# A transformer block on one core: the last two token tiles of the input products, with the other order of parts and one more tile transposed there

## The chip, the cores and the metric

The kernel runs on one core of a Trainium2 chip. The core has five engines with instruction streams of their own: TensorE (PE, matrix products and transposes), VectorE (DVE), ScalarE (ACT), GpSimd (POOL) and SyncE (SP, which issues DMAs here). [...] The metric is the time of one execution on the device in microseconds, and the median over runs is what counts.

## The reference

The computation is one block of a diffusion transformer, in float32, for 2 batches of 2048 tokens with 576 features: 16 heads of 36 dimensions and a hidden layer of 2304.

```python
mod = silu(c) @ w_ada + b_ada                    # six rows of 576 per batch
xn = ln(x) * (1 + sc_msa) + sh_msa
q, k, v = split(xn @ w_qkv + b_qkv)              # 576 -> 3 * 576
q, k = ln(q), ln(k)                              # over the 36 dimensions of each head
o = softmax(q @ k.T / sqrt(36)) @ v              # per head
x = x + g_msa * (o @ w_proj + b_proj)
h = gelu((ln(x) * (1 + sc_mlp) + sh_mlp) @ w1 + b1)
x = x + g_mlp * (h @ w2 + b2)
```

## The kernel before

**Stages.** For each batch the input products (`inputs`), the attention (`attend`) and the output product (`outputs`) follow one another; the hidden layer comes for both batches at the end. The change lies where the input products end and the attention opens, so it acts twice.

**Input products.** The 2048 tokens are 16 tiles of 128 (NT = 16, numbered 0 to 15). For each tile there are three products, q, k and v (w = 0, 1, 2), of 128 tokens by 576 features each, in two halves of 288 columns. The 576 input features are four chunks of 128 and one of 64. So a product has a part of 128 rows (`whole`, L376: eight matmuls) and a part of 64 rows (`halved`, L387: two matmuls, on the two halves of the array's rows). For tiles 0 to 13 a loop (L972) puts the 64-row parts of q, k and v together. The last two tiles have a loop of their own (L1005), in which `two_products` (L394) takes the two parts in an order by its argument `turn`: 128 rows first where it is even, 64 rows first where it is odd. Below, product number n = 3t + w: products 42, 43, 44 belong to tile 14, and 45, 46, 47 to tile 15.

**What follows a product.** `biased` (L957) takes it out of PSUM on VectorE. When q and k of a tile are there, `centred` (L879) subtracts each head's mean on VectorE and squares on ScalarE. Later `head_scale` (L894) sums the squares (VectorE), takes the square root (ScalarE, L903), the reciprocal (VectorE) and multiplies (POOL, L907). Then the rows are normalised, and `by_feature` (L912) transposes the nine chunks of q and k on TensorE (L917) and takes them out of PSUM: chunks 4 to 8 on VectorE (L926), chunks 0 to 3 on ScalarE (L922). For tile 15 `centred` runs for q behind product 45 and for k behind product 46, and `head_scale` follows at once.

**Keys for the attention.** When a block of tiles has been transposed, `by_feature` also issues DMAs on SP (`take_k_block`, L806) that copy the first pair's keys to the layout of the attention. The split of the last four dimensions (`parted`, L787, on VectorE) is put on the list `taken`, and runs at the end of the next call of `by_feature`. Tiles 12 and 13 are one such block, tiles 14 and 15 the next.

**The last two tiles before the change.** In tile 14, behind k (product 43), come the five transposes of tile 15's normed input (`input_by_feature`, L853, with five activations on ScalarE, L365) and the nine of tile 12. In tile 15, behind q (product 45), come the nine of tile 13. Tiles 14 and 15 are transposed inside the attention: `last` (L937) makes a call of `by_feature` for some chunks only, in which VectorE takes out all of them.

**The attention.** It goes by steps (p, qb, g): pair of heads, block of 512 queries, group of keys. In each step TensorE makes 16 score banks in two sets of eight matmul pairs (L1049), ScalarE takes the exponentials (L1053), and TensorE multiplies the exponentials of the step before by v (L1062). `hooks` (L1247) maps a step to something that is called in it behind the values: (0, 0, 0) tile 14's chunks 4 to 8, (0, 0, 1) tile 15's, (0, 1, 0) tile 14's chunks 0 to 3, (0, 1, 1) tile 15's. Keys of tiles 12 to 15 are read from g = 2 on, and the last query block from qb = 3.

**PSUM.** The eight banks are four tiles of two banks (`s_tile`) in the input products and eight single banks (`bank`) in the attention. An allocation waits until the last reader of what lay there has finished.

**Order.** TensorE runs in the order of the program text throughout. VectorE does so in `inputs` and `attend`, POOL in `attend`. The order on ScalarE is made by the framework's planner, which runs the program in its own reckoning of time and gives a free engine the earliest instruction of the text that is ready.

Of the kernel before, what the change touches and what calls it, by code (L numbers as in the profile page):

```python
# [23 lines left out]
NKC = FULL + 1  # L24
# [7 lines left out]
def dit_block(  # L32
# [30 lines left out]
    NT = N // P  # L63
# [7 lines left out]
    NQK = 2 * C // P  # L71
# [14 lines left out]
    def s_tile():  # L86
        return psum["s"].tile([P, 2, 512], F32, tag="s", name="s")
# [273 lines left out]
    def modulated(dst, src, which, b, apart=False):  # L361

        t4, t1 = transposed(*src, apart)
        for k in range(NKC):
            nc.scalar.activation(  # L365
                dst[:, k, :],
                t4[:, k * P : (k + 1) * P] if k < FULL else t1[:, :P],
                AF.Identity,
                bias=mod[:, which, k, b : b + 1],
                scale=mod[:, which + 1, k, b : b + 1],  # L370
            )
# [22 lines left out]
    def two_products(outs, stationary, moving, turn):  # L394


        parts = (whole, halved) if turn % 2 == 0 else (halved, whole)
        for part in parts:
            part(outs, stationary, moving, part is parts[0])
# [325 lines left out]
    def block_of_small():  # L725
# [34 lines left out]
        parts = ident.rearrange("p (r a b) -> p r a b", a=2, b=2)  # L760
# [8 lines left out]
        def chunk(c, cols):  # L769
            return qo[:, c, cols] if c < NKC else kr[:, c - NKC, cols]  # L770
# [42 lines left out]
        def take_q(p, qb):  # L813
            i = qb % 2
            src = lambda c: slice(qb * BLK, (qb + 1) * BLK)
            rows_taken(nc.sync, qm[i], qe[i], range(2), p * 2 * HD, src, slice(0, BLK))
            return lambda: parted(qe[i], slice(0, P), low_q, sign_q)
# [32 lines left out]
        def input_rows(b, t, queue):  # L850
            return tile_normed(tile_loaded(x[b, t * P : (t + 1) * P, :], queue))

        def input_by_feature(b, rows, apart=False):  # L853
            xnt = xs["pool"].tile([P, NKC, P], F32, name="xnt", bufs=2)
            modulated(xnt, rows, 0, b, apart)
            return xnt
# [13 lines left out]
        def inputs(b, weights, work, xnt, loaded):  # L870
# [5 lines left out]
            def banks_of_two():  # L876
                return [bank for ps in (s_tile(), s_tile()) for bank in (ps[:, 0], ps[:, 1])]
# [34 lines left out]
            def by_feature(t, banks, chunks=range(NQK), all_on_vector=False):  # L912
                both, begun = normed[t], [*taken]
                taken.clear()
                parts = [(c, banks[i // 4][:, i % 4 * P : i % 4 * P + P]) for i, c in enumerate(chunks)]
                for c, ps in parts:
                    nc.tensor.transpose(ps, both[:, c * P : (c + 1) * P], ident)  # L917

                for c, ps in parts[::-1]:
                    dst = chunk(c, slice(t * P, (t + 1) * P))  # L920
                    if c < 4 and not all_on_vector:
                        nc.scalar.activation(  # L922
                            dst, ps, AF.Identity, bias=bias_qk[:, c : c + 1], scale=gain_qk[:, c : c + 1]
                        )
                    else:
                        nc.vector.tensor_scalar(  # L926
                            dst, ps, gain_qk[:, c : c + 1], bias_qk[:, c : c + 1], ALU.mult, ALU.add
                        )
                for do in begun:
                    do()  # L930
                if t == TPB - 1:
                    taken.append(take_q(0, 0))
                if t + 1 in key_tiles and NQK - 1 in chunks:
                    i = key_tiles.index(t + 1)
                    taken.append(take_k_block(*key_tiles[i - 1 : i + 1]))
# [7 lines left out]
            def next_rows(t):  # L943
                return tile_normed(loaded.pop(0)) if loaded else input_rows(b, t, nc.sync)
# [25 lines left out]
            rows = next_rows(1)  # L970
            before = None
            for t in range(NT - 2):  # L972
# [11 lines left out]
                ahead = input_by_feature(b, rows, t in ((0, 9), (0, 1))[b])  # L984
                rows = next_rows(t + 2)
# [19 lines left out]
            for t in range(NT - 2, NT):  # L1005
                both = work.tile([P, 2 * C], F32, name="both", bufs=3)
                for w in range(3):
                    ps, parts = product(w, xnt)
                    two_products(*parts, 3 * t + w)
                    biased(w, ps, t, both)  # L1010
                    if w == 0:
                        head_scale(t - 1, before)

                    if w == (1 if t % 2 == 0 else 0):
                        if t + 1 < NT:
                            ahead = input_by_feature(b, rows)
                        by_feature(t - 2, banks_of_two())

                    if t == NT - 1 and w < 2:
                        centred(both, w, w + 1)  # L1020
                    if t == NT - 1 and w == 1:
                        head_scale(t, both, ((0, 1), (1, 2)))
                if t + 1 < NT:
                    centred(both)
                before, xnt = both, ahead
# [185 lines left out]
        for b in range(B):  # L1211
            work, close_work = opened("work", side="right")
            with tc.manual_schedule(engines={mybir.EngineType.DVE}):
                last_inputs = inputs(b, weights, work, xnt, loaded)
            close_weights()
            att, close_att = opened("att")
            close_psum()
            close_psum = opened_psum(b=8)
            km[1] = att.tile([P, N // 2], F32, name="km1")
            qm[1] = att.tile([P, BLK], F32, name="qm1")  # L1220
            opening = {}

            def last_inputs_done():
                last_inputs(NT - 1, range(NKC - 1))
                close_work()

            def ada_opened():
                opening["ada"], opening["close"] = opened("ada_later", 2, side="right")
                opening["was"] = ada_weights(opening["ada"], GATES[0])
                opening["gates"] = gate_biases(opening["ada"], GATES[0], GATES[2])  # L1230

            def ada_gates():
                gates(opening["was"], opening["gates"], *GATES[:2])
                opening["was"] = ada_weights(opening["ada"], LATER[0])
                opening["biases"] = feature_biases(opening["ada"], LATER[0], nc.sync)

            def ada_feature_rows():
                opening["rows"] = feature_rows(opening["ada"], opening["was"], opening["biases"])

            def ada_features():  # L1240
                features(opening["rows"], LATER[1])
                opening["close"]()

            def output_opened():
                opening["wp"] = output_weights(b)

            hooks = {  # L1247
                (0, 0, 0): lambda: last_inputs(NT - 2, range(NKC - 1, NQK)),
                (0, 0, 1): lambda: last_inputs(NT - 1, range(NKC - 1, NQK)),
                (0, 1, 0): lambda: last_inputs(NT - 2, range(NKC - 1)),  # L1250
                (0, 1, 1): last_inputs_done,
                (4, 0, 1): output_opened,
            }
            hooks |= {
                (3 + t // NBLK, t % NBLK, 3): lambda t=t: residual_begun(b, t) for t in range(NT + 1)
            }
            if b == 0:
                hooks |= {
                    (0, 2, 1): ada_opened,
                    (1, 0, 2): ada_gates,  # L1260
                    (2, 0, 2): ada_feature_rows,
                    (2, 0, 3): ada_features,
                }
            with tc.manual_schedule(engines={mybir.EngineType.DVE, mybir.EngineType.Pool}):
                attend(b, att, hooks)
            close_att()
            close_psum()
            close_psum = opened_psum(s=4)
            wp, close_wp = opening["wp"]
            if b + 1 < B:  # L1270
                weights, close_weights = input_weights()
                between = {
                    9: [lambda: opening.update(rows=input_rows(b + 1, 0, nc.scalar))],
                    14: [lambda: opening.update(xnt=input_by_feature(b + 1, opening["rows"]))],
                }
                outputs(b, wp, between, spare)
                xnt = opening["xnt"]
                close_wp()
# [373 lines left out]
```

## Time and profile before

| | |
|---|---|
| median of 3 runs | 3221.94 us (3221.2 to 3221.95) |
| the profiled execution | 3220.86 us, of which 3219.0 us from first to last instruction |
| TensorE / VectorE / ScalarE / POOL busy | 99% / 45% / 46% / 11% |
| granted clock of TensorE | 1.00 |
| tile 14 begins, batch 0 / 1 | 229.22 / 1319.55 us |
| first scores, batch 0 / 1 | 259.21 / 1349.55 us |
| first values, batch 0 / 1 | 266.30 / 1356.63 us |

In the profile L12 is line 12 of the kernel. A line of a timeline has the start in us, the length in us, the engine, the line, the operation, output and input, their shapes, and how many such instructions were merged; brackets hold the idle time of the engine ahead of it and what ended it. A float32 matmul counts as two instructions of TensorE, and lengths overlap there, so differences of starts are read. Values of a step's start are the mark that is used for the attention's pace: two of them lie 5.98 us apart where nothing stands between.

### The profile page before, as it was taken

The numbers are of one execution on the slowest core, as the hardware profiler recorded it, in microseconds if no ns is written. First come the engines' busy times: TensorE is split into PE (matmuls) and PEld (weight loads), VectorE is DVE, ScalarE is ACT, GpSimd is POOL, SyncE is SP. The second block draws the span as 40 slices with busy tenths as digits, with TensorE's granted clock in tenths as the row PEclk, the third lists the DMA queues.
The fourth block names the chain that finished last, engine by engine and source line by source line (L and its number), as shares of the span: only waits on it lengthen the run. The fifth ranks groups of instructions, "written<-read, shape, count | busy, mean of one in ns | idle before, by whom it ended". The sixth has DMA issues, their size and how long they took to land.

```text
span 3219.0 us, 46999 instructions
## 1 busy us (share of the span) xinstructions
PE 3199.1 (99%) x18143; PEld 1883.2 (59%) x18143; DVE 1452.6 (45%) x2131; ACT 1495.2 (46%) x2952; POOL 355.2 (11%) x432
## 2 busy tenths in 40 slices
PE   8999999999999999999999999999999999999999
PEld 6774333333333777633333333368888888777777
DVE  4674333333333367633333333345555444455454
ACT  2335666676666033466666667633555552000000
POOL 1111000112110111200001111010000000111111
PEclk9999999999999999999999999999999999999999
DMA  4102212223221401111222222154322223333321
GB/s 131 30 26 68 74 33 69 63 72 87 69 82 33 145 23 31 30 54 43 48 48 68 63 71 72 44 176 158 119 87 91 91 80 119 145 132 111 118 103 38
DMA packets 129332, 253.16 MB, mean 79 GB/s; under 512 B 22979, under 2 KB 68492, under 8 KB 127052
## 3 DMA queue, kind: packets, MB, share of 16 engines
q1 hardware_dynamic: 105588, 182.07, 18.5%
q0 software_dynamic: 22640, 66.23, 7.4%
q8 instruction: 145, 2.38, 0.3%
q10 hardware_dynamic: 872, 1.77, 0.2%
q14 instruction: 87, 0.71, 0.1%
HBM read 135.40 MB, written 66.35 MB: 63 GB/s over the span
## 4 chain that ended last, share of the span: by engine, by line
PE 99%; DMA 1%; SPq 0%; DVE 0%; issue 0%; ACT 0%; DVEq 0%
PE b L1062 28%; PE b L1049 19%; PE s L379 16%; PE s L1564 15%; PE m L1405 12%; PE s L390 2%; PE m L1419 2%; PE one L1405 2%; PE s L917 1%; PE s L357 1%; PE t L1465 0%; DMA wq<-in_w_qkv_dram 0%; PE b L192 0%; PE b L917 0%; DMA km<-qo 0%; PE s L358 0%
## 5 line engine op out<-in xcount | busy, mean ns | idle before, releaser
L1053 ACT ACTIVATE pt<-b 128x512 f32<-128x512 f32 x2048 | 1057.7, 610 | 485.4 <-PE b L1062 272.0
L1062 PE MATMUL b<-pt,vt 128*64 128x512 f32 x4096 | 935.0, 598 | 0.0
L1062 PEld LDWEIGHTS b<-pt,vt 128*64 128x64 f32 x4096 | 271.8, 136 | 582.0 <-issue 438.2
L1049 PE MATMUL b<-qm,km 32*128 32x512 f32 x4096 | 566.7, 614 | 0.3 <-DMA km<-qo 0.3
L1110 DVE TENSOR_TENSOR ot<-b,ot 128x512 f32<-128x512 f32 x192 | 132.8, 692 | 653.1 <-PE b L1062 652.6
L1049 PE MATMUL b<-qe,ke 16*128 16x512 f32 x2048 | 423.0, 790 | 0.0
L379 PE MATMUL s<-wq,xnt 128*128 128x288 f32 x1536 | 391.4, 408 | 1.9 <-DMA wq<-in_w_qkv_dram 1.1
L1564 PE MATMUL s<-ws,as 128*128 128x288 f32 x1440 | 351.8, 406 | 0.0
L1049 PEld LDWEIGHTS b<-qm,km 32*128 32x128 f32 x4096 | 191.7, 184 | 269.3 <-ACT pt L1053 206.8
L379 PEld LDWEIGHTS s<-wq,xnt 128*128 128x128 f32 x1536 | 284.6, 190 | 86.5 <-issue 13.5
L1564 PEld LDWEIGHTS s<-ws,as 128*128 128x128 f32 x1440 | 273.6, 190 | 75.6
L1081 DVE RECIPROCAL den<-den 128x512 f32<-128x512 f32 x64 | 213.5, 3337 | 12.0 <-DMA den<-den_dram 12.0
L1405 PE MATMUL m<-xnt,wb 128*128 128x256 f32 x864 | 213.8, 383 | 0.0
L1405 PE MATMUL m<-s,wb 128*128 128x256 f32 x864 | 210.1, 379 | 0.2 <-DVE s L1375 0.2
L1108 DVE COPY ot<-b 128x512 f32<-128x512 f32 x64 | 44.3, 692 | 334.7 <-PE b L1062 334.7
L1405 PEld LDWEIGHTS m<-xnt,wb 128*128 128x128 f32 x864 | 159.1, 190 | 32.2 <-issue 11.9
L1405 PEld LDWEIGHTS m<-s,wb 128*128 128x128 f32 x864 | 164.1, 190 | 22.9 <-DVE s L1375 0.6
L1049 PEld LDWEIGHTS b<-qe,ke 16*128 16x128 f32 x2048 | 108.2, 184 | 114.3 <-issue 113.1
L1432 DVE TENSOR_TENSOR cs<-m,cs 128x512 f32<-128x512 f32 x72 | 49.7, 691 | 212.3 <-ACT cs L1431 150.9
L1564 PE MATMUL s<-ws,hidden 128*128 128x288 f32 x576 | 142.3, 406 | 0.0
L1542 DVE TENSOR_TENSOR as<-hidden 128x1152 f32<-128x1152 f32 x80 | 139.1, 1802 | 0.0
L1443 ACT ACTIVATE cs<-cs,b_sb 128x512 f32<-128x512 f32 x144 | 98.8, 719 | 68.2 <-DVE cs L1438 31.4
(174 smaller groups left out, 2521.0 us busy)
## 6 DMA issues: line engine op xcount, KB each, us to landing
gelu<-cs SPq DMA_DIRECT2D x144, 256.0 KB
hidden<-gelu SPq DMA_DIRECT2D x16, 2304.0 KB
den<-den_dram SPq DMA_DIRECT2D x128, 128.0 KB
x_dram<-kr POOLq DMA_DIRECT2D x48, 288.0 KB, 2.8
qm<-qo SPq DMA_DIRECT2D x192, 64.0 KB
kr<-in_x_dram POOLq DMA_DIRECT2D x32, 288.0 KB, 3.8
xr<-x_dram SPq DMA_DIRECT2D x32, 288.0 KB
out_dram<-y POOLq DMA_DIRECT2D x30, 288.0 KB, 3.9
```

Source lines behind the costliest of these rows:

```text
L379: nc.tensor.matmul(outs[a], stationary(k, a), moving(k, a), start=(first and k == 0), stop=(not first and k == FULL - 1),)
L390: nc.tensor.matmul(outs[a], stationary(FULL, a)[r], moving(FULL, a)[r], start=first, stop=not first)
L1049: nc.tensor.matmul(ps, k[r, keys], q[r, :], start=first, stop=not first)
L1053: nc.scalar.activation(pt[:, h, :], banks[2 * c + h], AF.Exp, scale=SCALE)
L1062: nc.tensor.matmul(acc[64 * h : 64 * h + 64, :], vt[:, v0 : v0 + 64], pt[:, h, :], start=pt is pts[0][0], stop=pt is pts[-1][0],)
L1081: nc.vector.reciprocal(den, den)
L1110: nc.vector.tensor_tensor(ot, acc, ot, ALU.add)
L1405: nc.tensor.matmul(out_m[m], wb[:, slot[m], k, f * P : (f + 1) * P], moving[m](k), start=k == 0 and (m == 1 or (first and m in (2, 5, 6))) ...
L1419: nc.tensor.matmul(out_m[m], w[r, f * P : (f + 1) * P], a[r, FULL, t * PAIR : (t + 1) * PAIR], start=first and m != 4, stop=not first and ...
L1443: nc.scalar.activation(part, part, AF.Gelu, bias=b1_sb[:, g : g + 1])
L1542: nc.vector.tensor_tensor(stationary[m], x_, y_, op)
L1564: nc.tensor.matmul(ms[m], stationary[m][:, f, :], ws[m][:, f, :], start=(f == 0), stop=(f == HF - 1))
```

## The change

In the last two tiles `turn` is one higher, so that products 42, 44 and 46 begin with the 64-row part and 43, 45 and 47 end with it. The transposes move: tile 15's input and tile 12's q and k stand behind product 42 in place of 43, tile 13's behind 44 in place of 45. Tile 14's nine transposes stand behind product 46, ahead of `centred` for tile 15's k; ScalarE takes out four of the nine and VectorE five. The two hooks that transposed tile 14 in the attention are gone; tile 15's stay.

```diff
@@ -1006,15 +1006,15 @@
                 for w in range(3):
                     ps, parts = product(w, xnt)
-                    two_products(*parts, 3 * t + w)
+                    two_products(*parts, 3 * t + w + 1)
                     biased(w, ps, t, both)
                     if w == 0:
                         head_scale(t - 1, before)
 
-                    if w == (1 if t % 2 == 0 else 0):
-                        if t + 1 < NT:
-                            ahead = input_by_feature(b, rows)
-                        by_feature(t - 2, banks_of_two())
+                    if t == NT - 2 and w == 0:
+                        ahead = input_by_feature(b, rows)
+                    if 3 * t + w in (3 * NT - 6, 3 * NT - 4, 3 * NT - 2):
+                        by_feature(t - 2 + (w > 0), banks_of_two())
 
                     if t == NT - 1 and w < 2:
                         centred(both, w, w + 1)
@@ -1245,9 +1245,7 @@
             hooks = {
-                (0, 0, 0): lambda: last_inputs(NT - 2, range(NKC - 1, NQK)),
                 (0, 0, 1): lambda: last_inputs(NT - 1, range(NKC - 1, NQK)),
-                (0, 1, 0): lambda: last_inputs(NT - 2, range(NKC - 1)),
                 (0, 1, 1): last_inputs_done,
                 (4, 0, 1): output_opened,
             }
```

## The prediction

> **What bounds the kernel now.** I read the page first.
>
> ```profile
> span 3219.0 us, 46999 instructions
> PE 3199.1 (99%) x18143; PEld 1883.2 (59%) x18143; DVE 1452.6 (45%) x2131; ACT 1495.2 (46%) x2952; POOL 355.2 (11%) x432
> PE 99%; DMA 1%; SPq 0%; DVE 0%; issue 0%; ACT 0%; DVEq 0%
> ```
>
> TensorE carries 99% of the chain that ended last. Time is won or lost only as TensorE time, and a microsecond lost in the middle stays lost. The change acts at two places per batch, the end of the input products and the opening of the attention, so I read TensorE's order of time there, for batch 1 (batch 0 looks alike).
>
> ```profile
> 1335.36 4.15 PE L379 MATMUL s<-wq,xnt 128*128 128x288 f32 x16
> 1339.34 1.15 PE L917 MATMUL s<-ident,both 128*128 128x128 f32 x9
> 1340.33 4.05 PE L379 MATMUL s<-wq,xnt 128*128 128x288 f32 x16
> 1344.30 1.24 PE L390 MATMUL s<-wq,xnt 64*128 64x288 f32 x8
> 1345.47 4.15 PE L379 MATMUL s<-wq,xnt 128*128 128x288 f32 x16
> 1349.55 1.14 PE L1049 MATMUL b<-qm,km 32*128 32x512 f32 x8
> ...
> 1352.28 0.77 PE L917 MATMUL b<-ident,both 128*128 128x128 f32 x5
> ...
> 1356.63 3.65 PE L1062 MATMUL b<-pt,vt 128*64 128x512 f32 x16
> ...
> 1377.38 3.65 PE L1062 MATMUL b<-pt,vt 128*64 128x512 f32 x16
> 1380.97 0.66 PE L917 MATMUL b<-ident,both 128*128 128x128 f32 x4
> ...
> 1384.40 3.65 PE L1062 MATMUL b<-pt,vt 128*64 128x512 f32 x16
> ```
>
> From start to start: a 128-row part of a product takes 3.98 us, a pair of 64-row parts 1.17, nine transposes 0.98. Input products run without a gap up to the first scores at 1349.55. From there to the first values it takes 7.08 us, though a set of scores costs 2.40 in the steady state (304.43 to 306.83) and two sets plus five transposes (0.70) would be 5.5. So the opening has slack. Who sets it shows on ScalarE and VectorE:
>
> ```profile
> 1349.53 0.32 ACT L903 ACTIVATE var<-var,eps 128x32 f32<-128x32 f32 x1 [0.82 <-DVE var L897]
> 1349.87 1.28 ACT L1053 ACT_TABLE_LOAD   x1
> 1351.16 4.03 ACT L1053 ACTIVATE pt<-b 128x512 f32<-128x512 f32 x8
> ```
>
> ```profile
> 1340.22 1.34 DVE L897 TENSOR_REDUCE var<-sq 128x32 f32<-128x1152 f32 x1
> 1342.02 0.35 DVE L905 RECIPROCAL inv<-var 128x32 f32<-128x32 f32 x1 [0.46 <-ACT var L903]
> ...
> 1347.91 1.58 DVE L897 TENSOR_REDUCE var<-sq 128x16 f32<-128x576 f32 x2
> ```
>
> The square root of tile 15 (L903) comes first, then the table load for Exp, then eight exponentials that free the eight PSUM banks one by one; the second set of scores can end only behind the last. The first values start 5.47 us after the first exponential in both batches (1351.16 to 1356.63; 260.83 to 266.30). The opening is thus set by that square root, not by TensorE.
>
> [...] Here three 64-row parts take 1.66 us and two 1.17: 0.49 each and about 0.19 for a run, a small cost.
>
> **The change, part by part** (batch 1, W a 128-row part, H a 64-row part, T transposes).
>
> *Parity.* Before: WH HW WH HW WH HW. After: HW WH HW WH HW WH. Two single H stand at the ends in place of one pair: the same matmuls, one run more, about +0.1 us (0 to 0.2, from 0.19). I count an H at 0.58, half the pair.
>
> *Tile 14's nine transposes among the products.* +0.98 in the products. On the other side, five leave the opening (0.70) and four leave a later step. That step takes 7.02 us against 5.98 for its free neighbour (1371.40 to 1377.38): 1.04 saved (batch 0: 1.05). The five in the opening save nothing, since they stand inside the slack that the exponentials set; if they weren't covered it would be 0.70.
>
> *Input transposes of tile 15 and tile 12's transposes one product sooner.* Same instructions. Five ScalarE activations (1.85 us) start about 4 us sooner; product 44 then waits for their PSUM tile, which they leave some 2 us ahead of it. Counted at nothing; 0.6 us if the planner puts them behind tile 13's square root.
>
> *T13 one product sooner.* Five SP DMAs for keys of tiles 12 and 13 (1343.58 to 1347.14 in issue) go about 5 us sooner. Nothing else of SP's stands between. Their split on VectorE (0.85 us, from 1354.80) now follows tile 14's evictions, 12 us after tile 13's; for tile 15's block the same data came within 6.7 us (1362.34 to 1369.05). No wait.
>
> *The wait that T14 brings.* It needs tile 14's normalised rows, whose chain begins behind T13's evictions on VectorE. From T13's start:
> - VectorE, ScalarE, POOL: 1.19 to the first eviction (1329.23 to 1330.42), 1.71 for five, 1.60 for mean (1335.69 to 1337.29), 1.45 to the square, 1.20 to the sum of squares (1324.40 to 1325.60), 1.80 to the reciprocal, 0.49 to POOL (1342.51), 2.12 for its multiplication: 11.56 us.
> - TensorE: T13 0.98, product 45 W 3.98, HH 1.17, 46 W 3.98: 10.11 us.
>
> T14 therefore waits 1.45 us (0.5 to 2.5: no T14 in this place is in the trace, and eight terms of about 0.1 doubt each add up). Behind it stand product 47 and the scores. T13 begins 15.22 us into the stage (0.58+3.98+0.55+0.98+3.98+1.17+3.98), at 1334.77, so T14 at 1346.33 and the scores at 1346.33+0.98+3.98+0.58 = 1351.87, 2.32 late.
>
> *What is behind T14 on VectorE.* Its five evictions stand ahead of tile 15's key half (L885 to L887) and of its sum of squares. From T14's start: 1.19, 1.71, 0.85 for the split, 1.00 for the mean (1346.24 to 1347.24), 0.67 to the sums of squares, 1.62 to the square root, 1.63 to the first exponential: 8.67 us, so 1355.00 against 1351.16. The exponentials are **3.84 us late**, and they set the first values. The scores' own 2.32 are inside this. The last matmuls behind the eighth exponential may be shorter, as the two banks of the five transposes no longer come last: I take −0.2 (0 to −0.45).
>
> *Sum.* 3.84 − 0.2 − 1.04 = 2.6 us a batch. In batch 0 tile 14 starts at 229.22 in place of 1319.55 and the same sums give 264.67 against 260.83, again 3.84. Two batches: **+5.2 us**. Against the profiled execution's 3220.86 (span 3219.0 and 1.86 around it) that is 3226.1; the median of the runs is 1.1 above that execution, so 3221.94 + 5.2 = **3227.1 us**, 0.16% up. About 0.2% (6.4 us) is what a measurement tells from no change, so this counts as the same.
>
> **The rivals.**
> 1. *Exponentials ahead of the square root: slower.* ScalarE's order is the planner's. By my times the first exponential has its scores at 1351.87+1.45 = 1353.32 (1.45 as from 1374.98 to 1376.43), and the square root its sums at 1353.37. If in the planner's reckoning one exponential comes first, ScalarE loads Exp at once after the last square (1352.55, exponentials from 1353.85), then the square root's table, then Exp again: 1.28+0.32+1.28 = 2.88 more among the eight. They end at 1360.76 in place of 1359.03, 1.73 later a batch; 5.2+3.5 = 8.7, **3230.6 us**. It decides as soon as one exponential stands ahead. For it: a margin of 0.05 us. Against: before, the root came first, by 1.5 us.
> 2. *The opening doesn't hang on the exponentials.* Then only the scores' 2.32 count, less 0.70 and 1.04: 0.6 a batch, **3223.1 us**. Against it: 5.47 twice alike. For it: the eight exponentials could be taken up by later slack.
> 3. *Another wait*, such as a PSUM tile held by late ScalarE evictions (0.6 us above, or more): about 1.5 a batch more, 3230.
>
> **How the numbers follow.** My forecast 0.5, rival 1 0.3, rival 2 0.1, rival 3 0.1. The forecast's own range is 3225.5 to 3229, from the wait's bounds and the 0.45. The range 3223.0 to 3231.5 takes in rivals 1 and 2. Slower by over 0.2%: all of rival 1, 0.12 of the forecast, most of rival 3, 0.5. Faster: only if neither wait appears and all transposes saved count, 0.02. Same: 0.48.
>
> **What would show it.** In the changed profile: TensorE idle of about 1.5 us ahead of the L917 group between the last two 128-row parts of the products, put down to POOL L907; scores some 2.3 us later; one table load in the opening, some 3.8 later, or three (rival 1); first values 5.3 to 5.5 after the first exponential; one step of 7.0 fewer. The forecast is wrong if T14 finds its rows ready and the square root isn't late, or if the exponentials are late and the values aren't.

## The result, and the profile after

The changed kernel takes **3227.39 us** (median of 17 runs, 3226.73 to 3229.3) against 3221.80 us for the kernel before, measured beside it (17 runs, 3220.1 to 3223.07): +5.6 us or 0.17% by the medians. The ratio of all the runs is 1.0019, with a 95% interval of 1.0012 to 1.0026. That is slower, and just inside the 0.2% that were counted as no change.

The profiled execution of the changed kernel took 3228.63 us, 1.2 above its median; that of before was 0.9 below its own. The two profiles therefore lie 7.8 us apart where the medians lie 5.6 apart. The 7.8 divide as follows, by the start of the first input product of each batch (18.79 and 1111.15 us before, 19.88 and 1116.14 after): 1.1 ahead of any product, where nothing was changed, 3.9 in batch 0 and 2.8 from batch 1 on. The page of the changed kernel, its first two lines and the chain that ended last:

```profile
span 3226.8 us, 47001 instructions
PE 3202.7 (99%) x18143; PEld 1885.6 (58%) x18143; DVE 1454.2 (45%) x2123; ACT 1497.7 (46%) x2960; POOL 354.5 (11%) x432
...
PE 97%; DVE 2%; ACT 0%; DMA 0%; SPq 0%; issue 0%; DVEq 0%; ACTq 0%
```

There are as many matmuls as before, but VectorE now has 2% of the chain, where it had 0%. (That is how long the chain runs through VectorE, not what was lost there.) TensorE's order of time in batch 1 shows where (start, duration, instruction; in brackets the idle time ahead of it and what ended it):

```profile
1339.96 1.15 PE L917 MATMUL s<-ident,both 128*128 128x128 f32 x9
1340.94 4.05 PE L379 MATMUL s<-wq,xnt 128*128 128x288 f32 x16
1344.92 1.24 PE L390 MATMUL s<-wq,xnt 64*128 64x288 f32 x8
1346.09 4.15 PE L379 MATMUL s<-wq,xnt 128*128 128x288 f32 x16
1351.47 1.20 PE L917 MATMUL s<-ident,both 128*128 128x128 f32 x9 [1.24 <-POOL both L907]
1352.51 4.05 PE L379 MATMUL s<-wq,xnt 128*128 128x288 f32 x16
1356.49 0.76 PE L390 MATMUL s<-wq,xnt 64*128 64x288 f32 x4
1357.17 1.14 PE L1049 MATMUL b<-qm,km 32*128 32x512 f32 x8
...
1365.73 3.65 PE L1062 MATMUL b<-pt,vt 128*64 128x512 f32 x16
```

T13 (1339.96), T14 (1351.47) with 1.24 us of idle time ahead of it, the scores, the first values. On VectorE, in the same stretch:

```profile
1349.07 0.69 DVE L885 TENSOR_REDUCE sums<-both 128x16 f32<-128x576 f32 x1
1349.79 1.65 DVE L886 TENSOR_SCALAR sums<-sums 128x16 f32<-128x16 f32 x1
1351.48 0.76 DVE L887 TENSOR_TENSOR both<-both,sums 128x576 f32<-128x576 f32 x1
1352.16 0.75 DVE L960 TENSOR_TENSOR both<-s,bq 128x576 f32<-128x576 f32 x1
1352.83 1.36 DVE L926 TENSOR_SCALAR kr<-s,gb_qk 128x128 f32<-128x128 f32 x4
1354.10 0.40 DVE L926 TENSOR_SCALAR qo<-s,gb_qk 128x128 f32<-128x128 f32 x1
```

The second line is the one that I had not looked for: a scaling of 16 numbers in each partition takes 1.65 us, where it takes 0.17 us elsewhere. What releases it stands in POOL's order of time, and what it leads to in ScalarE's:

```profile
1349.29 2.12 POOL L907 TENSOR_TENSOR both<-both,inv 128x1152 f32<-128x1152 f32 x1 [14.06 <-PE s L379]
```

```profile
1358.74 0.32 ACT L903 ACTIVATE var<-var,eps 128x32 f32<-128x32 f32 x1 [0.82 <-DVE var L897]
1359.08 1.28 ACT L1053 ACT_TABLE_LOAD   x1
1360.37 5.00 ACT L1053 ACTIVATE pt<-b 128x512 f32<-128x512 f32 x10
```

POOL multiplies tile 14's rows from 1349.29 to 1351.41, and L886 ends at 1351.44. There is one table load, behind the square root of tile 15, and ten exponentials follow it without a gap. Counted from the start of tile 14 (1319.55 before, 1324.63 after), the square root comes 29.98 us into the stage before and 34.11 after, the first exponential at 31.61 and 35.74: 4.13 us late.

### The profile page after: what moved, and what is told of

Its sections match the earlier page's. It is cut to its first block, busy times and chain, and to the rows that moved or that the text cites. A ratio compares the mean times of both kernels' runs of the same rounds, so it can differ in the third digit from the quotient of the medians.

```text
span 3226.8 us, 47001 instructions
## 1 busy us (share of the span) xinstructions
PE 3202.7 (99%) x18143; PEld 1885.6 (58%) x18143; DVE 1454.2 (45%) x2123; ACT 1497.7 (46%) x2960; POOL 354.5 (11%) x432
## 4 chain that ended last, share of the span: by engine, by line
PE 97%; DVE 2%; ACT 0%; DMA 0%; SPq 0%; issue 0%; DVEq 0%; ACTq 0%
PE b L1062 28%; PE b L1049 19%; PE s L1562 15%; PE s L379 14%; PE m L1403 12%; PE m L1417 2%; PE s L390 2%; PE one L1403 2%; PE s L917 1%; PE s L357 0%; PE t L1463 0%; DVE both L887 0%; DMA wa<-in_w_ada_dram 0%; DVE kr L926 0%; DVE sums L885 0%; PE b L192 0%
```

## The experiments

Two theories stood after the result. **W**: TensorE's wait ahead of T14 is what makes the opening late, as the prediction had it. **L**: VectorE is late by itself, since its own order of work has changed. Times "into the stage" are counted from the start of tile 14, as above, and come from the one profiled execution of each kernel. The experiments also ask which part of the change costs what. T12, T13 and so on are the transposes of those tiles; "the root" is the square root of tile 15.

**Is it the root that the opening hangs on?** In the kernel before, the two sums of squares of tile 15 are taken twice:

```
-                        head_scale(t, both, ((0, 1), (1, 2)))
+                        head_scale(t, both, ((0, 1), (1, 2), (0, 1), (1, 2)))
```

> The kernel before, with tile 15's two sums of squares taken twice on VectorE (1.58 us more ahead of its square root); TensorE's work is untouched. Theory A: first exponential and first values 1.6 us later in each batch, +3.2 us in all. Theory B: no change, 0 us.

Measured: 3223.81 us against 3221.18, ratio 1.0008 (1.0001 to 1.0015), +2.6. VectorE's order of time in this kernel:

```profile
1351.62 2.90 DVE L897 TENSOR_REDUCE var<-sq 128x16 f32<-128x576 f32 x4
```

It was 1.58 for two, so the two extra sums took 1.32 us and not the 1.58 that were expected. The root is 1.37 later in both batches (31.35 into the stage for 29.98), the first values are 1.37 later as well (38.45 for 37.08), and the time follows. The other side of the same claim is that five transposes in the opening cost nothing. They were left out of the kernel before, and the places that they would fill were zeroed:

```
-                (0, 0, 0): lambda: last_inputs(NT - 2, range(NKC - 1, NQK)),
+                (0, 0, 0): lambda: last_inputs(NT - 2, range(0)),
```

> The kernel before without tile 14's five transposes and evictions in the opening (its chunks 4 to 8 stay zero; the split of the keys of tiles 12 and 13 stays where it was). Theory A (the opening hangs on the exponentials behind tile 15's square root, so these five are hidden): 0 to -0.8 us against the kernel before, the latter if the last scores' tail is 0.4 us shorter a batch. Theory B (TensorE's own work sets the opening): -1.4 us.

Measured: 3221.39 against 3221.34, ratio 0.9999 (0.9991 to 1.0008), 0.0. That interval is some 5 us wide, so the time alone doesn't tell the two theories apart, and the trace shows that the run is no clean test. VectorE and ScalarE have in batch 1

```profile
1349.55 0.35 DVE L792 TENSOR_SCALAR high<-ke,part 64x256 fp32r<-64x256 f32 x1 [0.18 <-DMA ke<-kr]
```

```profile
1352.36 5.00 ACT L1055 ACTIVATE pt<-b 128x512 f32<-128x512 f32 x10
```

The split of the keys of tiles 12 and 13 (L792) did not stay where it was: it now runs between tile 15's two sums of squares, although it stands behind them in the program text, and puts the root off, by 0.44 us in batch 0 and 0.47 in batch 1. The first values come 0.33 and 0.36 us later than before, although TensorE has five transposes less to do. Behind the first exponential they come after 5.35 us in place of 5.47. So 0.12 of the 0.70 us show, and the rest lay inside the slack: the first values again follow the exponentials, and not TensorE's work.

**Wait or order?** In the changed kernel, T14 reads tile 13's rows, which have long been there, so TensorE need not wait:

```
-                both, begun = normed[t], [*taken]
+                both, begun = normed[t - 1 if t == NT - 2 else t], [*taken]
```

> The change, but tile 14's transposes read tile 13's rows, which are long ready (wrong values for tile 14): TensorE doesn't wait for POOL. Theory W (that wait is what makes everything behind it late): scores and square root about 1.4 us earlier a batch, -2.5 us against the change, so +3 us over the kernel before. Theory L (VectorE is held as long anyway, in the scaling of tile 15's sums, L886, which took 1.65 us in place of 0.17 and ended with POOL's multiplication of tile 14): scores 1.3 us earlier, square root and first exponential as late as in the change, time as the change, +5 to +5.6 us.

Measured: 3227.55 against 3221.34, ratio 1.0022 (1.0013 to 1.0031), +6.2: nothing is won. TensorE's, VectorE's and ScalarE's orders of time of this kernel:

```profile
1350.07 1.15 PE L917 MATMUL s<-ident,both 128*128 128x128 f32 x9
```

```profile
1349.80 1.66 DVE L886 TENSOR_SCALAR sums<-sums 128x16 f32<-128x16 f32 x1
```

```profile
1359.09 1.28 ACT L1053 ACT_TABLE_LOAD   x1
```

T14 starts 1.40 us sooner and the idle time ahead of it is gone, but L886 still takes 1.66 and the table load stands at 1359.09, where the change has it at 1359.08; in both batches the root is as far into the stage as in the change, within 0.02 us. W as it stands falls: the loss doesn't need TensorE's wait.

**Is it POOL's multiplication that holds VectorE?** In the changed kernel POOL multiplies the first half of tile 14 alone (the q half; k stays unscaled):

```
+                n = H if t == NT - 2 else 2 * H
-                    heads, heads, inv.unsqueeze(2).to_broadcast([P, 2 * H, HD]), ALU.mult
+                    heads[:, :n], heads[:, :n], inv[:, :n].unsqueeze(2).to_broadcast([P, n, HD]), ALU.mult
```

> The change, with POOL multiplying only the q half of tile 14 (its keys stay unscaled): 1.06 us less of POOL. Theories W and L both: transposes of tile 14, square root and first values 1.06 us earlier a batch, -2.1 us against the change. If something else holds VectorE and TensorE there (the PSUM tiles, the DMAs of the keys): 0.

Measured: 3225.54 against 3221.34, ratio 1.0013 (1.0006 to 1.0019), +4.2; 1.4 to 1.9 less than the change (by the differences, or by the medians themselves). POOL's and VectorE's orders of time here:

```profile
1345.27 1.15 POOL L908 TENSOR_TENSOR both<-both,inv 128x576 f32<-128x576 f32 x1 [14.06 <-PE s L379]
```

```profile
1345.77 0.68 DVE L886 TENSOR_SCALAR sums<-sums 128x16 f32<-128x16 f32 x1
```

POOL's operation ends at 1346.42, and L886 at 1346.45. Its length follows POOL's end. The interval overlaps that of the change, so the times alone don't prove the gain, but the traces have it: the root is 0.96 and 0.98 us earlier into the stage in batches 0 and 1 (34.09 and 33.13, for 35.05 and 34.11). Both theories had asked for that, as POOL releases T14 as well.

**What do tile 14's evictions cost?** In the changed kernel ScalarE takes all nine of them, so that none stands ahead of the root on VectorE:

```
-                    if c < 4 and not all_on_vector:
+                    if (c < 4 or t == NT - 2) and not all_on_vector:
```

> The change, with all nine chunks of tile 14 taken out of PSUM on ScalarE, so that only the split of the keys stands ahead of tile 15's keys on VectorE. If the evictions on VectorE are what puts the square root off (my step of 1.71 us): the square root waits for the last square on ScalarE behind nine evictions of 0.37 us in place of it, about 1 us earlier a batch, -2 us against the change. If they are not: 0 or slower than the change.

Measured: 3225.16 against 3221.34, ratio 1.0011 (1.0005 to 1.0018), +3.8, so 1.8 to 2.2 less than the change (again with overlapping intervals). TensorE's and ScalarE's orders of time:

```profile
1349.16 1.20 PE L917 MATMUL s<-ident,both 128*128 128x128 f32 x9 [1.24 <-POOL both L907]
```

```profile
1355.24 0.32 ACT L903 ACTIVATE var<-var,eps 128x32 f32<-128x32 f32 x1 [0.82 <-DVE var L897]
```

The wait ahead of T14 is still 1.24, but from T14 to the root it takes 6.08 us in place of 7.27, and the first values come 1.17 us sooner into the stage (39.93 for 41.10). Again the time follows the root and not TensorE's wait.

**Which part of the change makes VectorE meet POOL?** First the change without tile 14: the parity, and T12, T13 and the input transposes of tile 15 a product sooner.

```
-                    two_products(*parts, 3 * t + w)
+                    two_products(*parts, 3 * t + w + 1)
...
+                    if 3 * t + w in (3 * NT - 6, 3 * NT - 4):
+                        by_feature(t - 2 + (w > 0), banks_of_two())
```

> The other parity, and the transposes of tiles 12 and 13 and of tile 15's input one product sooner; tile 14 stays in the attention as before. Theory A (the loss comes from tile 14's transposes, through their wait and through tile 15's square root behind their evictions): a single run of 64-row parts more and a wait of product 43 for its PSUM tile in batch 0, 0.2 and 0.9 us, so 0.5 to 1.5 us over the kernel before, and one table load in the opening as late as before. Theory P (the single runs of 64-row parts cost most of it): 3 us or more over the kernel before.

Measured: 3229.25 against 3221.18, ratio 1.0026 (1.0016 to 1.0037), +8.1. Theory A had it too low. The number lies where theory P put it, 3 us or more, but theory P's reason still has to be tested. The orders of time of VectorE, POOL, ScalarE and TensorE:

```profile
1348.83 1.65 DVE L886 TENSOR_SCALAR sums<-sums 128x16 f32<-128x16 f32 x1
...
1355.96 0.69 DVE L963 TENSOR_TENSOR vt<-s,bq 128x576 f32<-128x576 f32 x1
```

```profile
1348.33 2.13 POOL L907 TENSOR_TENSOR both<-both,inv 128x1152 f32<-128x1152 f32 x1 [14.06 <-PE s L379]
```

```profile
1355.27 0.32 ACT L903 ACTIVATE var<-var,eps 128x32 f32<-128x32 f32 x1 [0.82 <-DVE var L897]
1355.61 1.28 ACT L1053 ACT_TABLE_LOAD   x1
1358.22 4.03 ACT L1053 ACTIVATE pt<-b 128x512 f32<-128x512 f32 x8 [1.33 <-PE b L1049]
```

```profile
1356.71 1.12 PE L1049 MATMUL b<-qm,km 32*128 32x512 f32 x5 [2.88 <-DVE vt L963]
```

Two things happen. L886 is held here too, with no T14 among the products at all, and the root is 1.63 us late (31.61 into the stage for 29.98). Then the exponentials wait 1.33 more, for scores that TensorE could not write: TensorE stands 2.88 us, until VectorE has added the value bias (L963), which frees the PSUM tile of product 47. Together the first exponential is 2.95 us late (34.56 for 31.61).

Is it the parity or the order? The order alone, with the parity of before:

```
-                    if w == (1 if t % 2 == 0 else 0):
-                        if t + 1 < NT:
-                            ahead = input_by_feature(b, rows)
-                        by_feature(t - 2, banks_of_two())
+                    if t == NT - 2 and w == 0:
+                        ahead = input_by_feature(b, rows)
+                    if 3 * t + w in (3 * NT - 6, 3 * NT - 4):
+                        by_feature(t - 2 + (w > 0), banks_of_two())
```

> Before's parity, with the transposes of the change for tiles 12 and 13 and tile 15's input (behind products 42 and 44 in place of 43 and 45); tile 14 stays in the attention. Theory L (with tile 13's evictions earlier, VectorE reaches the scaling of tile 15's sums while POOL multiplies tile 14, and stands 1.5 us): the square root 1.5 us late, at least +3 us, and up to the +8 us of the parity kernel if the first scores' PSUM tile comes as late. Theory P (the other parity is what costs): +1 us or less, for two runs of 64-row parts more.

Measured: 3231.13 against 3220.76, ratio 1.0033 (1.002 to 1.0045), +10.4. VectorE's order of time shows the same stall:

```profile
1351.00 1.65 DVE L886 TENSOR_SCALAR sums<-sums 128x16 f32<-128x16 f32 x1
```

So it is the order, and theory P falls: it allowed 1 us. But +10.4 is also more than the 8 that theory L allowed. In this kernel TensorE ran at half its clock for a while in both openings (in batch 1 score matmuls that take 0.79 to 0.82 us elsewhere take 1.41; see the last section): from the first exponential to the first values it takes 7.45 and 6.50 us in place of 5.47, 3.0 us in all that neither theory had. And the change without tile 14, with POOL's multiplication of tile 14 halved as above:

> The parity kernel (tile 14 in the attention) with POOL multiplying only the q half of tile 14. Theory L: VectorE is held 1.06 us less a batch, square root, product 47's bias and with it the first scores' PSUM tile that much earlier, -2.1 us against the parity kernel, +6 over the kernel before. If POOL has no part in the parity kernel's loss: no change, +8 us.

Measured: 3226.50 against 3220.76, ratio 1.002 (1.0011 to 1.0028), +5.7, which is 2.3 to 2.8 less than without the halving. These two intervals overlap as well. In the traces L886 takes 0.68 us in place of 1.65, and the root is 0.96 us earlier into the stage in both batches (31.59 and 30.65, for 32.55 and 31.61). There is no T14 among the products here, so this is VectorE's own hold, apart from TensorE's wait.

**Tile 14 elsewhere.** Three places were tried. In the first, the kernel before keeps its parity and order, and tile 14's nine transposes stand behind product 47, all evicted on VectorE, with the hooks of tile 14 removed:

```
+                    if t == NT - 1 and w == 2:
+                        by_feature(t - 1, banks_of_two(), all_on_vector=True)
...
-                (0, 0, 0): lambda: last_inputs(NT - 2, range(NKC - 1, NQK)),
...
-                (0, 1, 0): lambda: last_inputs(NT - 2, range(NKC - 1)),
```

> Before's parity; tile 14's nine transposes behind product 47, behind tile 15's norm on VectorE, all taken out on VectorE; none in the attention. Theory A (the opening hangs on the first exponential): the square root is as early as before, the scores start 0.98 us later, and the first exponential stands 1.45 us behind them, 0.8 us late; 1.04 us saved in the later step: -0.2 us a batch, -0.5 us in all (-1.5 to +1). Theory B (the opening hangs on TensorE's own work): 0.98 - 0.70 - 1.04 = -0.8 us a batch, -1.5 us.

Measured: 3226.58 against 3221.18, ratio 1.0016 (1.0009 to 1.0024), +5.4; both expectations missed. TensorE's and ScalarE's orders of time:

```profile
1355.23 1.12 PE L1051 MATMUL b<-qm,km 32*128 32x512 f32 x2 [0.68 <-DVE kr L926]
...
1357.77 0.77 PE L1051 MATMUL b<-qm,km 32*128 32x512 f32 x3 [1.43 <-DVE qo L926]
```

```profile
1353.81 1.28 ACT L1055 ACT_TABLE_LOAD   x1
1359.43 5.15 ACT L1055 ACTIVATE pt<-b 128x512 f32<-128x512 f32 x10 [4.34 <-PE b L1051]
```

The root is in time, yet the first exponential waits 4.34 us for scores, which wait for PSUM tiles that tile 14's transposes hold until VectorE has evicted them.

In the second, the changed kernel issues T14 behind tile 15's means and squares:

```
-                    if 3 * t + w in (3 * NT - 6, 3 * NT - 4, 3 * NT - 2):
+                    if 3 * t + w in (3 * NT - 6, 3 * NT - 4):
...
+                        by_feature(t - 1, banks_of_two())
```

> The change, but tile 14's transposes stand behind tile 15's norm in the text: TensorE's order stays that of the change with the wait for POOL, while VectorE takes tile 14 out of PSUM only after tile 15's sums of squares. Theory A: the square root comes in time again, the first exponential follows the scores (2.4 us later than before) by 1.45 us, so about 2.3 us late in place of 4.1; less 1.2 saved: 1.1 us a batch and 0.9 for batch 0's PSUM wait, about +3 us over the kernel before, 2.5 us under the change. Theory B: the same as the change, +5.6 us, as TensorE's order and waits are the same.

Measured: 3229.91 against 3221.18, ratio 1.0029 (1.0018 to 1.004), +8.7; both missed. L886 is held here too, and the root came 31.60 us into the stage, as in the change without tile 14 (31.61). But TensorE's order of time has

```profile
1358.92 1.66 PE L1050 MATMUL b<-qm,km 32*128 32x512 f32 x5 [2.92 <-ACT qo L922]
```

a wait for a PSUM tile of tile 14 that ScalarE evicts late. On ScalarE those four evictions also stand ahead of the table load for Exp, which comes 3.90 us behind the root in place of 0.34.

In the third, the kernel before does all nine in the opening, where five cost nothing:

```
-                (0, 0, 0): lambda: last_inputs(NT - 2, range(NKC - 1, NQK)),
+                (0, 0, 0): lambda: last_inputs(NT - 2, range(NQK)),
...
-                (0, 1, 0): lambda: last_inputs(NT - 2, range(NKC - 1)),
```

> The kernel before, with all nine of tile 14's transposes in the opening's first step; the later step of four is gone. The opening has slack for TensorE (five of them cost nothing there), so the later step's 1.04 us are saved. Against it: nine evictions on VectorE (some 3 us) hold three PSUM banks that the second set of scores needs. If the slack takes them: -2 us; if the banks hold the scores: -2 us plus about 0.7 a batch, -0.6 us or nothing.

Measured: 3220.98 against 3220.76, ratio 0.9998 (0.999 to 1.0006), the same. From the first exponential to the first values it takes 6.65 us for 5.47, +1.18, and the later step that loses its four transposes gives 1.04 back. That is the second of the two cases expected. None of the kernels tried was faster than the kernel before.

## Why the prediction was right, and where a step of it failed

The time was right: 3227.1 forecast, 3227.39 measured, within the forecast's own range of 3225.5 to 3229. At +5.6 of the 6.4 us that 0.2% make, it lies near the bound between the same and slower, as the even chances for the two had it. The reasons were right in part only. Step by step, forecast against the two batches of the profiled execution:

| step | forecast | batch 1 | batch 0 |
|---|---|---|---|
| tile 14's start to T13 | 15.22 | 15.33 | 16.28 |
| T13 to T14 | 11.56 | 11.51 | 11.51 |
| idle ahead of T14 | 1.45 | 1.24 | 1.24 |
| T14 to scores | 5.54 | 5.70 | 5.70 |
| T14 to first exponential | 8.67 | 8.90 | 8.90 |
| first exponential to first values | 5.27 | 5.36 | 5.96 |
| saved in later steps | 1.04 | 1.24 | 1.20 |

**What held.** "*The opening is thus set by that square root, not by TensorE*" is shown from both sides: with a root 1.37 later the first values come 1.37 later, and with five transposes fewer they still follow the first exponential, 0.12 us sooner behind it. With that the five in the opening save next to nothing, and rival 2 falls. It holds while the first scores find their PSUM tiles free; where they don't, as in five of the kernels above, the opening waits for the scores (the first exponential by 0.93 to 4.34 us in their batch 1). Rival 1 did not come about: one table load, the root ahead of the exponentials. Rival 3 came in small, and in one batch: product 43 of batch 0 waited 0.69 us for a PSUM tile that VectorE had not yet freed, as this line of TensorE's order of time shows.

```profile
237.77 4.15 PE L379 MATMUL s<-wq,xnt 128*128 128x288 f32 x16 [0.69 <-DVE both L960]
```

That is most of batch 0's 1.06 in the table's first row. Waits of this kind were larger (in batch 1 2.88 us for L963 and 2.92 us for L922, above) in the experiments that moved tile 14 or the order, and made much of their loss.

**What failed.** The step that failed is *T13 one product sooner*, which was given "No wait". *The wait that T14 brings* was there, 1.24 us for 1.45, but it is not by itself what makes the root late. Without it the time stayed, and without T14 the root was late all the same, by 1.63 us. In the kernel before, VectorE and POOL have

```profile
1342.29 1.27 DVE L926 TENSOR_SCALAR kr<-s,gb_qk 128x128 f32<-128x128 f32 x4
1343.47 0.40 DVE L926 TENSOR_SCALAR qo<-s,gb_qk 128x128 f32<-128x128 f32 x1
1343.79 0.74 DVE L885 TENSOR_REDUCE sums<-both 128x16 f32<-128x576 f32 x1
1344.57 0.17 DVE L886 TENSOR_SCALAR sums<-sums 128x16 f32<-128x16 f32 x1
```

```profile
1342.51 2.12 POOL L907 TENSOR_TENSOR both<-both,inv 128x1152 f32<-128x1152 f32 x1 [12.48 <-PE s L379]
```

After the reciprocal for tile 14 come T13's evictions, which read PSUM. They run beside POOL's multiplication (to 1344.63) and take 1.27 us for four and 0.40 for one, no longer than the 1.36 and 0.40 of tile 14's in the change (1352.83), where POOL stands still. Then come tile 15's mean and its L886, which takes 0.17 us as POOL ends. With T13 a product sooner its evictions come ahead of tile 14's chain, and VectorE goes from the reciprocal straight to tile 15's mean and L886, into POOL's multiplication. L886 then lasts until POOL is done: 1.48 us more. The lengths show it: L886 ended 0.03 us behind POOL in the change, and its length followed POOL's from 1.65 down to 0.68 when the multiplication was halved; the tensor_reduce L885 ran into the same multiplication (1349.07 to 1349.76) in 0.69, no longer than the 0.75 of its next call (1355.44), with POOL at rest. Why the one is held and the other is not, no trace shows.

Counted along VectorE's order, the lateness of 4.13 us in batch 1 is then 1.48 for L886 and 2.61 for tile 14's five evictions and the split ahead of tile 15's key half (1352.83 to 1355.44), 4.09. The forecast put 1.45 on TensorE's wait and 2.4 on the rest, and its 8.67 from T14 on was 8.90. The number came out right because the same operation of POOL releases both T14 on TensorE and L886 on VectorE, 0.03 us apart: whichever of the two is followed, the clock starts at the same end. The prediction did not see the second hold, so that it came so near is in part luck, and a reader who had removed the wait, as was tried, would have won nothing.

Nor would removing the other hold alone win much in the changed kernel. The prediction's 1.19 us from transposes to first eviction would put T14's evictions at 1351.47 + 1.19 = 1352.66; VectorE, held by L886, came to them at 1352.83. By this estimate the change would gain 0.17 us a batch if L886 were free and TensorE still waited. The two holds run side by side, and each is enough for nearly all of the delay: VectorE's as the run without TensorE's wait shows, TensorE's by this estimate.

**What the parts cost.** The order alone, with the new parity, costs no less than the whole change (+8.1 and +5.6; the intervals overlap). In batch 1 of the profiles the two are alike: first values 2.95 late there, against 4.02 late less 1.24 saved, 2.78, in the change. So T14 among the products about pays for itself. By the traces that is because in the change the first scores no longer wait for L963: TensorE stands for it 0.79 us, but later in the first set of scores, where no exponential waits. (What the single runs of 64-row parts cost beside this is small: they take 0.68 to 0.69 us each, where the prediction counted 0.58.) The order, which the prediction counted at nothing, is without tile 14 enough for a loss as large as the whole.

**Sizes.** In the profiled execution batch 1 lost 2.87 us from the start of T11 to the sixth values, for 2.6; batch 0 lost 4.46. Of the 1.59 that batch 0 lost more, 0.95 is the later T13 (16.28 for 15.33) and 0.60 lies between the first exponential and the first values, where TensorE ran at half its clock (0.50 granted for some 3.4 us, below).

**Open.** Which PSUM tile the first scores inherit is settled by the allocation and by what was moved; it was read from the waits and not varied by itself. L886 without POOL but with TensorE's wait was not tried either: in the change, halving the multiplication shortens both. So the 0.17 us above is an estimate and not measured.

## What to carry to other kernels

Moving work earlier changes what stands behind it on each engine: ask which instruction now falls beside a GpSimd operation, and how long it takes there and apart from it. Here L886 took 1.65 us in place of 0.17, where the evictions that had stood there took no longer (1.27 us for four). Look at lengths as well as at waits: the hold of L886 shows in the trace as an instruction of ten times its usual length (1.65 us for 0.17), and its line has no bracket, as nothing counts it as a wait. An idle stretch that a trace names on the bounding engine is a symptom until its removal is tried; a second engine may be held by the same release, and then removing one hold alone can win nothing, as here (3227.55 us without TensorE's wait, 3227.39 with it). At a change of stage, look at which PSUM tile the first allocation of the next stage takes over, and who frees it last: in the change without tile 14 TensorE stood 2.88 us for that.

## What was not expected of the hardware

A [128, 16] tensor_scalar in SBUF (L886) took 0.17 us alone and 1.65 us where it started 0.50 us into a GpSimd tensor_tensor of 2.12 us; in the change and in the seven experiments in which it met that operation (halved in two of them, where it took 0.68 us) it ended 0.02 to 0.03 us behind it. A larger one was held too: a [128, 576] tensor_scalar (L279) took 1.90 us beside POOL in batch 0 of the kernel before and of the changed one, ending 0.3 us behind POOL, and 0.58 alone.

TensorE's granted clock fell from 1.00 to 0.50 in the opening of batch 0 of the changed kernel, some 2 us behind a wait of 0.79 us. The columns of the view by stretches are: stretch, length, busy time of PE, PEld, DVE, ACT and POOL with their counts, PE's clock, DMA share, GB/s.

```profile
266.00:268.00 2.00, 1.21 (x11) 0.50 (x10) 0.97 (x2) 1.97 (x4) 1.31 (x1) 1.00 0.31 73
268.00:270.00 2.00, 2.00 (x15) 1.49 (x11) 0.00 (x0) 2.00 (x6) 2.00 (x4) 0.78 0.09 20
270.00:272.00 2.00, 2.00 (x17) 2.00 (x13) 0.00 (x0) 1.79 (x4) 0.99 (x2) 0.50 0.71 121
272.00:274.00 2.00, 2.00 (x15) 0.97 (x9) 0.00 (x0) 0.73 (x2) 0.00 (x0) 0.86 0.41 55
```

In stretches of 0.50 us the clock reads 0.64 from 269.00 on, then six times 0.50, then 0.95, and 1.00 on both sides. Taken as full or half throughout, it was at half for 0.88 + 2.00 + 0.56 = 3.44 us by the stretches above, and for 0.36 + 3.00 + 0.05 = 3.41 by the shorter ones. What set this off the trace does not show: no gap of the 30 us before was longer than 1.24 us, and batch 1, with the same two gaps of 1.24 and 0.79 us, kept its 1.00. It cost 0.60 us here, as the table above has it.

The experiments show the same. Counted in the same way by stretches of 2 us, there is a spell of 3.40 to 3.44 us at half clock in batch 1's opening of the order alone (with the parity of before) and in both openings of three others (T14 on tile 13's rows, T14 behind product 47, T14 behind tile 15's norm; in batch 1 of this last one the clock reads 0.85, 0.50 and 0.80 in the three stretches from 1358.00 to 1364.00, so 0.60 + 2.00 + 0.80 us). Batch 0 of the order alone and of the change without tile 14 with POOL halved has one of 6.84 us, twice as long; in the latter the first values come 7.51 us behind the first exponential in place of 5.47. There is none in the openings of the kernel before and of the other experiments, the change without tile 14 among them, in which TensorE had stood still for 2.88 us. So a gap of that size came without a spell there. Why one opening was taken and another not stays open, and whether these spells have a part in the spread between executions was not measured.
